# Decoder layer on one core: the first entry's loads in halves, and no idle products between its transposes

## The chip, the cores and the metric

The kernel runs on one core of a Trainium2 chip. The metric is the time of one execution on the device, in microseconds (us). The core has engines that work side by side, each on its own row of instructions: TensorE (PE) for matrix products, VectorE (DVE), ScalarE (ACT), GpSimd (POOL), and SyncE (SP), which here only issues DMAs. ACT issues a few DMAs too. PE loads its stationary operand with a separate instruction, shown as PEld, which overlaps the products. The line numbers below are those of the profile of the kernel before.

## The reference

One decoder layer with B = 4 entries of the batch, 512 rows each, D = 512 and 16 heads of 32, all in float32. Cut to what matters:

```python
x = x + attention(layernorm(x), q_w, q_b, k_w, k_b, v_w, v_b, o_w, o_b)   # causal
x = x + cross_attention(layernorm(x), ctx, ctx)                           # causal, no weights
x = x + ffn(layernorm(x), W_up, W_down, W_gate, W_expert)
# ffn: relu(x @ W_up.T) @ W_down.T + (sum of the softmaxed top-2 gates) * (x @ W_expert)
```

For the first projection of an entry, the rows are normalised (mean and variance over D), and q = xn @ q_w.T + q_b, k = xn @ k_w.T + k_b. The change concerns only how the first entry gets there.

## The kernel before, in words

An entry is 512 x 512 and is held in four row blocks of 128 (NT = 4); the weights are held with the contracted dimension on the partitions in four chunks of 128 (NC = 4). Everything stays on one core, and the four entries follow one another. PE, DVE, ACT and POOL run in exactly the order in which the program writes their instructions (`manual_schedule`, line 947); SP issues the DMAs in program order too, and a DMA may have to wait until an earlier one has landed, because eight completion semaphores are used in turn.

The start, ahead of the loop over entries:

1. `load_x(0)` (lines 70 to 76) issues four DMAs, one per block of 256 KB: blocks 0 and 2 from SP, 1 and 3 from ACT. Then SP issues wq and wk, each in two pieces by row chunks (`load_w(..., 2)`, lines 85 to 91, 104 and 105), then the biases, wv, the context of entry 0 (cv), wo, wup, wdown, wgate, wexp.
2. POOL makes constants, `ident` (the unit matrix) among the first. PE runs `keep_warm("warm", 12)` (line 949, products at line 179), which multiplies `ident` by itself 12 times into a scratch PSUM tile. Nobody reads it.
3. `norm_in(0, x0)` (line 558): for each block, `stats` (lines 189 to 201: `bn_stats` and `bn_aggr` on DVE, then on POOL `ve` and `rstd` as a power of -0.5), and after all four of them `normal` for each block (line 206 on DVE).
4. `turn(0)` and `turn(2)` (line 573) call `columns` (line 245): the transposes of two blocks, four instructions each (line 251), into one PSUM tile of two banks, and then one ACT copy of both (line 257) into `xnT`, the transposed normalised rows. For the first entry `columns` calls `keep_warm` with 2 ahead of each block's four transposes.
5. `query_key(e)` (line 590): for each feature block f of 128, four products for query (line 235, 128 x 512) and four for key, then ACT adds the biases (lines 604 and 607). For the first entry, f = 0 is done in two halves of the rows: `half(n)` (line 615) multiplies 256 columns of `xnT` by wq's chunks and then by wk's; the first half needs only the first ACT copy of step 4.

The first four of these steps (`skip`, line 958: two halves of f = 0, query and key of f = 1) run ahead of attention; the others are the filler that `with_maxima` (line 865) puts between the score products of the first attention. There DVE also reads `xin`, the blocks of the next entry, which SP loads after the weights. Float32 products appear in the profile as two PE instructions each; a transpose is one.

PSUM tiles come from one pool of four buffers (`pair`, line 65), used in turn.

```python
    def keep_warm(name, count):
        out = pair(name)
        for n in range(count):
            nc.tensor.matmul(
                out[:, 0, :P], lhsT=ident, rhs=ident, start=True, stop=True
            )
```

Of the kernel before, what the change touches and what calls it, by code (L numbers as in the profile page):

```python
# [9 lines left out]
F32 = mybir.dt.float32  # L10
# [8 lines left out]
P = 128  # L19
# [7 lines left out]
def decoder_layer(  # L27
# [21 lines left out]
    nc = tc.nc  # L49
    B, S, D = x.shape  # L50
# [3 lines left out]
    NC = D // P  # L54
# [4 lines left out]
    const = ctx.enter_context(tc.tile_pool(name="const", bufs=1))  # L59
# [5 lines left out]
    def pair(name):  # L65

        return ps.tile([P, 2, S], F32, tag="ps", name=name)


    def load_x(b):  # L70
        xb = act.tile([P, NT, D], F32, tag="x", name=f"x_{b}", bufs=2)
        src = x[b].rearrange("(t p) d -> p t d", p=P)
        for t in range(NT):
            queue = nc.scalar if b == 0 and t % 2 else nc.sync
            queue.dma_start(out=xb[:, t, :], in_=src[:, t, :])
        return xb

    def load_cv(b):
# [3 lines left out]
            nc.sync.dma_start(out=cv[:, t, :], in_=src[:, t, :])  # L82
        return cv

    def load_w(ap, name, parts=1):
        w = const.tile([P, NC, ap.shape[-1]], F32, tag=name, name=name)
        src = ap.rearrange("(c p) o -> p c o", p=P)
        for n in range(parts):
            c = slice(n * NC // parts, (n + 1) * NC // parts)
            nc.sync.dma_start(out=w[:, c, :], in_=src[:, c, :])  # L90
        return w

    def load_b(ap, name):
# [7 lines left out]
        return t  # L101

    x0 = load_x(0)
    wq_sb = load_w(wq, "wq_sb", 2)
    wk_sb = load_w(wk, "wk_sb", 2)
    bk_sb = load_b(bk, "bk_sb")
    bq_sb = load_b(bq, "bq_sb")
    wv_sb = load_w(wv, "wv_sb")
# [27 lines left out]
    for r in range(HG):  # L136
# [8 lines left out]
    warm = const.tile([P, 1], F32, name="warm")  # L145
# [14 lines left out]
        out=nfloor,  # L160
        in_=nfloor,
# [7 lines left out]
    parts = []  # L169
    for n in range(2):  # L170
        t = const.tile([P, NT, P], BF16, name=f"parts{n}")
# [3 lines left out]
# [7 lines that stand above are left out]
# [60 lines left out]
            if c < NC - 1:  # L242
                yield

    def columns(srcs, dst, t, tp, scale=None, warm=0):

        for n, src in enumerate(srcs):
            if warm:
                keep_warm(f"warm_{t}_{n}", warm)
            for c in range(NC):  # L250
                nc.tensor.transpose(  # L251
                    tp[:, n, c * P : (c + 1) * P], src[:, c * P : (c + 1) * P], ident
                )
        to = dst[:, :, t * P : (t + 2) * P].rearrange("p c (n q) -> p c n q", q=P)
        come = tp.rearrange("p n (c q) -> p c n q", q=P)
        if scale is None:
            nc.scalar.copy(to, come)
        else:
            nc.scalar.mul(to, come, scale)
# [298 lines left out]
    def norm_in(b, given=None):  # L558

        e = Entry()  # L560
        e.b, e.x, e.xn_t = b, given, None
        src = x[b].rearrange("(t p) d -> p t d", p=P)

        def source(t):
            if given is not None:
                return given[:, t, :]
            xi = work.tile([P, D], F32, tag="xin", name=f"xin_{b}_{t}")
            nc.sync.dma_start(out=xi, in_=src[:, t, :])
            return xi

        made, norms = layernorms(source, f"a{b}", ahead=given is not None)

        def turn(t):
            if e.xn_t is None:
                e.xn_t = act.tile([P, NC, S], F32, tag="xn_t", name=f"xnT_{b}")
            columns(
                [made[t], made[t + 1]],
                e.xn_t,
                t,
                pair(f"tp_a{b}_{t}"),  # L580
                warm=0 if b else 2,
            )

        return e, norms, [(lambda t=t: turn(t)) for t in (0, 2)]
# [5 lines left out]
    def query_key(e):  # L590
        b, made = e.b, {}
        e.q_t = act.tile([P, NC, S], F32, tag="q_t", name=f"qT_{b}")
        e.k_t = act.tile([P, NC, S], F32, tag="k_t", name=f"kT_{b}")

        def query(f):
            made[f] = pair(f"pm_qk{b}_{f}")
            yield from project_t(made[f][:, 0, :], wq_sb, e.xn_t, f)

        def key(f):
            yield from project_t(made[f][:, 1, :], wk_sb, e.xn_t, f)  # L600
            out(f)

        def out(f):
            nc.scalar.activation(
                e.k_t[:, f, :], made[f][:, 1, :], AF.Identity, bias=bk_sb[:, f : f + 1]
            )
            nc.scalar.activation(
                e.q_t[:, f, :],
                made[f][:, 0, :],
                AF.Identity,  # L610
                bias=bqs_sb[:, f : f + 1],
                scale=SCALE,
            )

        def half(n):

            if n == 0:
                made[0] = pair(f"pm_qk{b}_0")
            rows = slice(n * S // 2, (n + 1) * S // 2)
            for u, w in enumerate((wq_sb, wk_sb)):  # L620
                for c in range(NC):
                    nc.tensor.matmul(
                        made[0][:, u, rows],
                        lhsT=w[:, c, :P],
                        rhs=e.xn_t[:, c, rows],
                        start=(n == 0 and c == 0),
                        stop=(n == 1 and c == NC - 1),
                        skip_group_check=True,
                    )
            if n == 1:  # L630
                out(0)

        steps = [(lambda f=f, w=w: w(f)) for f in range(NC) for w in (query, key)]
        if b == 0:
            steps[:2] = [lambda: half(0), lambda: half(1)]
        return steps

    def value(e):
# [308 lines left out]
    with tc.manual_schedule(engines=BY_HAND):  # L947
        e, norms, turns = norm_in(0, x0)
        keep_warm("warm", 12)
        run(norms)  # L950
        run(turns)
        nc.gpsimd.tensor_scalar(bqs_sb, bq_sb, SCALE, None, ALU.mult)
        nc.vector.tensor_reduce(
            fold, ident.rearrange("p (c e) -> p e c", e=HD), axis=AX.X, op=ALU.add
        )
        add_bias(e)
        between_self = query_key(e) + value(e)
        skip, between_cross, ahead = 4, [], []
        for b in range(B):
            more = b + 1 < B  # L960
            sa = Attention(e.q_t, e.k_t, e.v, False, f"s{b}")
            norms, turns = [], []
            if more:
                after, norms, turns = norm_in(b + 1)
            late = with_maxima(between_self, sa, skip, norms)
            if b == B - 1:
                e.x = load_x(b)
            attend(sa, late)
            if b > 0:
                add_bias(e)  # L970
            made = out_projection(e, sa, context(e) + turns)
            steps = (query_key(after) if more else []) + between_cross
            run(steps[:2])
            norm_cross(e, made, 0)
            run(steps[2:3])
            norm_cross(e, made, 2)
            ca = Attention(e.cq_t, e.ck_t, e.cv, True, f"c{b}")
            ca.e, ca.out = e, e.beh_t
            late = with_maxima(steps[3:], ca)
            if b + 2 < B:  # L980
                after.x = load_x(b + 1)
            attend(ca, late)
            if more:
                cvs[b + 1] = load_cv(b + 1)
            filler = value(after) if more else ahead
            run(filler[:1])
            made = add_cross(e, ca)

            fill = matmuls(filler[1:])
            for t, k in ((0, 8), (2, 2)) if b != B - 2 else ((0, 12), (2, 0)):  # L990
                for _ in range(k):
                    next(fill)
                norm_ffn(e, made, t)
            for _ in fill:
                pass
            gates, ups, downs, experts = ffn(e)
            if b + 3 < B:
                between_self, between_cross = gates[:1] + ups + gates[1:] + downs, experts
            elif b + 2 < B:
                between_self, between_cross = gates[:1] + ups + gates[1:] + downs, []  # L1000
                ahead = experts
            elif more:
                between_self, ahead = ahead + ups[:2], experts
                between_cross = gates[:1] + ups[2:] + gates[1:] + downs
            else:
                run(gates[:1] + ups + gates[1:])
                run(downs[:2] + experts[:2] + downs[2:] + experts[2:])
            skip = 0
            if more:
                e = after  # L1010
# [48 lines left out]
```

## Time and profile before

| | us |
|---|---|
| median of 3 runs (809.56 to 809.82) | 809.8 |
| the profiled execution, its own time | 809.92 |
| its span, first to last instruction | 808.2 |
| PE busy | 796.8 |
| DVE busy | 563.7 |
| ACT busy | 395.4 |
| POOL busy | 332.8 |
| first instruction of PE | 1.52 |
| first product of query (line 622) | 11.59 |
| first attention's first score products (line 286) | 27.18 |

The span is the time between the first and the last instruction of one execution under the profiler; the execution's own time is 1.7 us longer. Starts are counted from the beginning of the span. In the rows of a timeline the first number is the start, the second the busy time, then come engine, line, operation, the tile written and the tiles read, their shapes, the number of merged instructions, and in brackets how long the engine had been idle and what ended that. The busy time of a PE row includes the pipeline's tail, so rows that follow each other overlap a little: the distance between starts is the better measure of what a product costs. The trace records the landing of each DMA and its single packets as well; where it is said that a DMA landed so many us after its issue, that is from its row in the table of DMA issues.

### The profile page before, as it was taken

The numbers are of one execution on the slowest core, as the hardware profiler recorded it, in microseconds if no ns is written. First come the engines' busy times: TensorE is split into PE (matmuls) and PEld (weight loads), VectorE is DVE, ScalarE is ACT, GpSimd is POOL, SyncE is SP. The second block draws the span as 40 slices with busy tenths as digits, with TensorE's granted clock in tenths as the row PEclk, the third lists the DMA queues.
The fourth block names the chain that finished last, engine by engine and source line by source line (L and its number), as shares of the span: only waits on it lengthen the run. The fifth ranks groups of instructions, "written<-read, shape, count | busy, mean of one in ns | idle before, by whom it ended". The sixth has DMA issues, their size and how long they took to land. (4 is left out here: it accounts for less than half of the span.)

```text
span 808.2 us, 13950 instructions
## 1 busy us (share of the span) xinstructions
PE 796.8 (99%) x5616; PEld 379.9 (47%) x5616; DVE 563.7 (70%) x957; ACT 395.4 (49%) x448; POOL 332.8 (41%) x523
## 2 busy tenths in 40 slices
PE   8999999999999999999999999999999999999998
PEld 7444454444444454444544445444444454434444
DVE  2478865879678854588867786688859766988512
ACT  2457526861546515566045752686056824674110
POOL 4334612554234732266333482266423653465100
PEclk9999999999999999999999999999999999999999
DMA  9601000001001000020100000000102000000101
GB/s 337 236 28 28 1 1 1 2 2 53 1 27 27 2 1 0 2 77 29 53 14 14 1 2 1 0 2 1 54 26 79 2 2 0 1 2 2 52 1 52
DMA packets 13680, 24.50 MB, mean 30 GB/s; under 512 B 1968, under 2 KB 2224, under 8 KB 13616
## 3 DMA queue, kind: packets, MB, share of 16 engines
q1 hardware_dynamic: 13184, 22.96, 8.4%
q8 instruction: 44, 0.72, 0.4%
q10 hardware_dynamic: 432, 0.66, 0.2%
q14 instruction: 20, 0.16, 0.1%
HBM read 19.42 MB, written 4.19 MB: 29 GB/s over the span
## 5 line engine op out<-in xcount | busy, mean ns | idle before, releaser
L317 DVE TENSOR_REDUCE nm_s<-s_s 128x2 f32<-128x1024 f32 (+3 forms) x128 | 97.0, 811 | 35.2 <-POOL s_s L305 35.2
L317 DVE TENSOR_REDUCE nm_c<-s_c 128x2 f32<-128x1024 f32 (+3 forms) x128 | 95.8, 810 | 31.0 <-POOL s_c L305 31.0
L297 ACT COPY s_s<-sm_s 128x1024 f32<-128x1024 f32 x80 | 77.1, 1015 | 70.7 <-PE sm_s L286 36.4
L297 ACT COPY s_c<-sm_c 128x1024 f32<-128x1024 f32 x80 | 77.1, 1016 | 35.9 <-PE sm_c L286 16.2
L305 POOL TENSOR_SCALAR_AFFINE_SELECT s_c<-s_c 128x512 f32<-128x512 f32 (+1 forms) x80 | 43.9, 550 | 100.4 <-ACT s_c L297 100.4
L305 POOL TENSOR_SCALAR_AFFINE_SELECT s_s<-s_s 128x512 f32<-128x512 f32 (+1 forms) x80 | 43.8, 551 | 97.1 <-ACT s_s L297 97.1
L423 ACT ACTIVATE pt_c<-sc_c 128x1024 f32<-128x1024 f32 x64 | 61.7, 1031 | 21.0 <-PE sc_c L400 15.4
L510 DVE TENSOR_TENSOR sum_s<-sum_s,pt_s 128x256 f32<-128x256 f32 (+2 forms) x72 | 59.8, 895 | 16.7 <-PE pv_s L462 16.7
L431 POOL TENSOR_SCALAR_AFFINE_SELECT pt_c<-pt_c 128x512 f32<-128x512 f32 (+1 forms) x64 | 51.1, 806 | 27.0 <-ACT pt_c L423 26.6
L223 PE MATMUL pm_d<-wdown_sb,hT 128*128 128x512 f32 x128 | 61.5, 610 | 0.0
L423 ACT ACTIVATE pt_s<-sc_s 128x1024 f32<-128x1024 f32 x56 | 53.9, 1030 | 12.6 <-PE sc_s L400 7.0
L235 PE MATMUL pm_u<-fT,wup_sb 128*128 128x512 f32 x128 | 59.3, 604 | 0.0
L223 PE MATMUL pm_v<-wv_sb,xnT 128*128 128x512 f32 x128 | 58.8, 600 | 0.0
L687 PE MATMUL pm_o<-wo_sb,oT_s 128*128 128x512 f32 x128 | 57.8, 596 | 0.0
L235 PE MATMUL pm_qk<-xnT,wk_sb 128*128 128x512 f32 x120 | 57.3, 607 | 0.0
L389 PE MATMUL sc_c<-cqT,ckT 32*128 32x384 f32 (+3 forms) x512 | 56.0, 464 | 1.4 <-ACT sum_c L423 0.8
L235 PE MATMUL pm_qk<-xnT,wq_sb 128*128 128x512 f32 x120 | 56.7, 604 | 0.0
L223 PE MATMUL pm_e<-wexp_sb,fT 128*128 128x512 f32 x120 | 56.3, 604 | 0.0
L389 PE MATMUL sc_s<-qT,kT 32*128 32x128 f32 (+3 forms) x512 | 54.4, 462 | 1.2 <-ACT sum_s L423 0.9
L431 POOL TENSOR_SCALAR_AFFINE_SELECT pt_s<-pt_s 128x512 f32<-128x512 f32 (+1 forms) x56 | 48.1, 868 | 17.6 <-ACT pt_s L423 17.0
L286 PE MATMUL sm_c<-ckT,cqT 32*128 32x512 f32 (+3 forms) x512 | 47.5, 460 | 0.0
L286 PE MATMUL sm_s<-kT,qT 32*128 32x512 f32 (+3 forms) x512 | 47.0, 461 | 0.0
(164 smaller groups left out, 1269.3 us busy)
## 6 DMA issues: line engine op xcount, KB each, us to landing
cv<-in_ctx_dram SPq DMA_DIRECT2D x16, 256.0 KB, 4.0
out_dram<-x SPq DMA_DIRECT2D x15, 256.0 KB, 2.0
x<-in_x_dram SPq DMA_DIRECT2D x14, 256.0 KB, 4.1
xin<-in_x_dram SPq DMA_DIRECT2D x12, 256.0 KB, 2.7
wq_sb<-in_wq_dram SPq DMA_DIRECT2D x2, 512.0 KB, 6.2
wk_sb<-in_wk_dram SPq DMA_DIRECT2D x2, 512.0 KB, 7.8
wv_sb<-in_wv_dram SPq DMA_DIRECT2D x1, 1024.0 KB, 8.3
wo_sb<-in_wo_dram SPq DMA_DIRECT2D x1, 1024.0 KB, 9.7
```

The lines of the kernel that those rows point to most:

```text
L223: nc.tensor.matmul(pm, lhsT=lhs_t[:, c, t * P : (t + 1) * P], rhs=w[:, c, :], start=(c == 0), stop=(c == NC - 1),)
L235: nc.tensor.matmul(pm, lhsT=w[:, c, f * P : (f + 1) * P], rhs=rhs_t[:, c, :], start=(c == 0), stop=(c == NC - 1),)
L286: nc.tensor.matmul(scs[r // 2][:, r % 2, c : c + (i + 1) * P], lhsT=self.q_t[h, g, i * P : (i + 1) * P], rhs=self.k_t[h, g, : (i + 1) * P] ...
L297: nc.scalar.copy(s, scs[n])
L305: nc.gpsimd.affine_select(out=diagonal, in_=diagonal, compare_op=ALU.is_ge, fill=NEG, base=0, pattern=[[0, 2], [0, len(pieces)], [-1, P]], ...
L317: nc.vector.tensor_reduce(self.nm[g][:, i, 2 * n : 2 * n + 2], made[n][:, :, c : c + (i + 1) * P], axis=AX.X, op=ALU.max, negate=True,)
L389: nc.tensor.matmul(scs[r // 2][:, r % 2, c : c + S - j * P], lhsT=self.k_t[h, g, j * P : (j + 1) * P], rhs=self.q_t[h, g, j * P :], start= ...
L423: nc.scalar.activation(pt, scs[n], AF.Exp)
L431: nc.gpsimd.affine_select(out=diagonal, in_=diagonal, compare_op=ALU.is_ge, fill=0.0, base=0, pattern=[[0, 2], [0, len(pieces)], [1, P]], ...
L510: nc.vector.tensor_tensor(to, to, pts[n][:, :, c : c + S - j * P], ALU.add)
L687: nc.tensor.matmul(pms[t // 2][:, t % 2, :], lhsT=a.out[:, c, t * P : (t + 1) * P], rhs=wo_sb[:, c, :], start=(c == 0), stop=(c == NC - 1),)
```

## The change

- Blocks 0 and 1 of the first entry's x are each loaded by two DMAs of 256 columns (128 KB), the left half from SP, the right half from ACT. Blocks 2 and 3 are loaded whole, from SP and from ACT.
- wq and wk are loaded by column halves, in the order wq left, wk left, wq right, wk right. The left half has the columns of f = 0 and 1.
- The idle products between the transposes go; the 12 ahead of them stay.
- For f = 0 only query is done in two halves of the rows; key is done whole, as for the other f. There are five steps ahead of attention instead of four, with the same content.

```diff
         for t in range(NT):
-            queue = nc.scalar if b == 0 and t % 2 else nc.sync
-            queue.dma_start(out=xb[:, t, :], in_=src[:, t, :])
+            if b > 0:
+                nc.sync.dma_start(out=xb[:, t, :], in_=src[:, t, :])
+            elif t > 1:
+                (nc.sync, nc.scalar)[t % 2].dma_start(out=xb[:, t, :], in_=src[:, t, :])
+            else:
+
+                for n, queue in enumerate((nc.sync, nc.scalar)):
+                    half = slice(n * D // 2, (n + 1) * D // 2)
+                    queue.dma_start(out=xb[:, t, half], in_=src[:, t, half])
...
-    def load_w(ap, name, parts=1):
+    def load_w(ap, name):
         w = const.tile([P, NC, ap.shape[-1]], F32, tag=name, name=name)
-        src = ap.rearrange("(c p) o -> p c o", p=P)
-        for n in range(parts):
-            c = slice(n * NC // parts, (n + 1) * NC // parts)
-            nc.sync.dma_start(out=w[:, c, :], in_=src[:, c, :])
+        nc.sync.dma_start(out=w, in_=ap.rearrange("(c p) o -> p c o", p=P))
...
-    wq_sb = load_w(wq, "wq_sb", 2)
-    wk_sb = load_w(wk, "wk_sb", 2)
+
+    wq_sb, wk_sb = (const.tile([P, NC, D], F32, name=name) for name in ("wq_sb", "wk_sb"))
+    for cols in (slice(0, D // 2), slice(D // 2, D)):
+        for w, ap in ((wq_sb, wq), (wk_sb, wk)):
+            nc.sync.dma_start(
+                out=w[:, :, cols], in_=ap.rearrange("(c p) o -> p c o", p=P)[:, :, cols]
+            )
...
-    def columns(srcs, dst, t, tp, scale=None, warm=0):
+    def columns(srcs, dst, t, tp, scale=None):
 
         for n, src in enumerate(srcs):
-            if warm:
-                keep_warm(f"warm_{t}_{n}", warm)
             for c in range(NC):
...
-                warm=0 if b else 2,
...
-            for u, w in enumerate((wq_sb, wk_sb)):
-                for c in range(NC):
-                    nc.tensor.matmul(
-                        made[0][:, u, rows],
-                        lhsT=w[:, c, :P],
-                        rhs=e.xn_t[:, c, rows],
-                        start=(n == 0 and c == 0),
-                        stop=(n == 1 and c == NC - 1),
-                        skip_group_check=True,
-                    )
-            if n == 1:
-                out(0)
+            for c in range(NC):
+                nc.tensor.matmul(
+                    made[0][:, 0, rows],
+                    lhsT=wq_sb[:, c, :P],
+                    rhs=e.xn_t[:, c, rows],
+                    start=(n == 0 and c == 0),
+                    stop=(n == 1 and c == NC - 1),
+                    skip_group_check=True,
+                )
...
-            steps[:2] = [lambda: half(0), lambda: half(1)]
+            steps[:1] = [lambda: half(0), lambda: half(1)]
...
-        skip, between_cross, ahead = 4, [], []
+        skip, between_cross, ahead = 5, [], []
```

## The prediction

> **What bounds the kernel now.** I read the page's busy times first: they say which engine a saving has to reach.
>
> ```profile
> PE 796.8 (99%) x5616; PEld 379.9 (47%) x5616; DVE 563.7 (70%) x957; ACT 395.4 (49%) x448; POOL 332.8 (41%) x523
> ```
>
> PE is idle for only 808.2 - 796.8 = 11.4 us. The same static order runs from the first projection to the end, so whatever lets PE start that row earlier should move the end by as much, if nothing on another engine or a queue arrives too late for the earlier PE. Then the timeline of PE, DVE and ACT over the first 19 us (start, busy time, engine, line, tiles, count, idle before it):
>
> ```profile
> 1.52 5.22 PE L179 MATMUL warm<-ident 128*128 128x128 f32 x28 [1.52 <-POOL ident masks.py:199]
> 8.45 0.66 PE L251 MATMUL tp_a<-ident,xn_a 128*128 128x128 f32 x4 [1.71 <-DVE xn_a L206]
> 8.94 0.61 PE L179 MATMUL warm<-ident 128*128 128x128 f32 x4
> 9.39 0.60 PE L251 MATMUL tp_a<-ident,xn_a 128*128 128x128 f32 x4
> 9.82 0.61 PE L179 MATMUL warm<-ident 128*128 128x128 f32 x4
> 10.27 0.60 PE L251 MATMUL tp_a<-ident,xn_a 128*128 128x128 f32 x4
> 10.71 0.61 PE L179 MATMUL warm<-ident 128*128 128x128 f32 x4
> 11.15 0.60 PE L251 MATMUL tp_a<-ident,xn_a 128*128 128x128 f32 x4
> 11.59 1.89 PE L622 MATMUL pm_qk<-xnT,wq_sb 128*128 128x256 f32 x8
> ...
> 4.66 0.69 DVE L194 BATCH_NORM_STATS2 st_a<-x 128x6 f32<-128x512 f32 x1 [4.66 <-DMA x<-in_x_dram]
> 7.88 2.04 DVE L206 TENSOR_SCALAR xn_a<-x,mv_a,rs_a 128x512 f32<-128x512 f32 x4
> ...
> 10.02 1.01 ACT L257 COPY xnT<-tp_a 128x1024 f32<-128x1024 f32 x1 [6.82 <-PE tp_a L251]
> 11.79 1.01 ACT L257 COPY xnT<-tp_a 128x1024 f32<-128x1024 f32 x1 [0.75 <-PE tp_a L251]
> ```
>
> What the reader should see: DVE starts at 4.66, released by the DMA of x, and then has no idle time; four statistics steps of 0.80 us and the four normalisations follow each other. PE waits 1.71 us for the first normalised block, then runs without a gap, so from 8.45 on it is PE's own work that sets the 11.59, and three of its seven pieces there (8.94, 9.82, 10.71) compute nothing. From 11.59 to 18.50 PE does block 0 of query and key.
>
> Last, the clock, because the idle products touch it. Within the first group (line 179) the starts of single products are 0.213 us apart until about 5.4 us and 0.111 us apart after it. The stretches around the end show the other direction (the PEclk column is the third from the right):
>
> ```profile
> 5.38:8.79 3.41, 1.70 (x15) 1.00 1.05 397
> 8.79:12.21 3.42, 3.42 (x30) 1.00 1.07 371
> 804.10:807.51 3.41, 0.42 (x2) 1.00 0.23 77
> 807.51:808.10 0.59, 0.00 (x0) 0.50 0.00 0
> ```
>
> The clock record goes to full rate at 5.38 us and to half at 807.51: 802.13 us, 235 times 3.413 us, so it is decided in steps of 3.41 us. A step with 0.42 us of PE work ended in half clock, one with 1.70 us (5.38 to 8.79) did not.
>
> **The change, part by part.**
>
> *Idle products.* Sixteen go (two before each of four transpose groups, two instructions each). The first four end the first group and lie in PE's wait for DVE: nothing saved. The other three sets take 0.45, 0.45 and 0.44 us on PE's path, 1.33 us together. Not all of that is gained, since DVE and ACT come next. The single normalisations end at 8.39, 8.85, 9.30 and 9.92 (the fourth starts late, at 9.375, because POOL's rs_a ends at 9.34). A group of four transposes takes 0.44 us and starts 0.06 us after its block. So the groups start at 8.45, 8.94 (behind the first group), 9.38 and 9.98. ACT's first copy started 0.63 us after the start of the second group (9.39 to 10.02), so now 8.94 + 0.63 = 9.57, and with 1.01 us and 0.06 us to PE the first product of query can start at 10.65. The new last arrival is that copy, not PE's last transpose (10.42). The second copy: 9.98 + 0.63 + 1.01 = 11.62, needed after the first half of query, 10.65 + 1.73 = 12.38: covered by 0.76 us. Gain 11.59 - 10.65 = 0.94 us.
>
> *x in halves.* Now blocks 0 and 1 are on two queues that share the DMA engines, and land together: by the packet records block 0's last completion is at 4.27, block 1's at 4.35, and DVE starts 0.40 us after the former. In steady flow a 2 KB packet takes 0.084 us and an engine carries eight for each block, alternating. In halves the first sixteen packets of an engine are all block 0, 1 KB each. The only 1 KB packets of this trace (the last output) take 0.046 us. Sixteen of those save 16 x (0.084 - 0.046) = 0.6 us against sixteen of 2 KB; slow first packets (0.3 to 1.0 us) stay. Block 0 would be usable at about 4.1. Block 1 comes 16 x (2 x 0.046 - 0.084) = 0.13 us later than now, at about 4.9, and its statistics would be due at 4.9. Block 2's last completion is at 5.40, usable at 5.80, with the same 0.13 us 5.93; due at 6.29 - 0.6 = 5.7. So block 2 becomes the late one, and the chain gains 6.29 - 5.93 = 0.36 to 6.29 - 5.80 = 0.49 us. I take 0.40. Ends: 0 if slow first packets are paid per packet (sixteen either way), 0.6 if block 2 comes earlier too. Below nothing is bounded by block 1: were it 0.3 us later than reckoned, it still starts before 5.49.
>
> Here a rule speaks against the change: the Trainium skill, "DMA: Bandwidth & Descriptors", section "Issuing engines are not separate DMA queues", says that DMAs of different issuing engines run on the same 16 engines and interleave, and that issuing from several saves only sequencer time. By that rule the halves give nothing, and the sum is 0.97. The two completions 0.09 us apart show the interleaving; but both kernels use two queues, and what changes is which bytes go first. So I keep 0.40.
>
> *Weights by column halves.* Before, query's block 0 needs all of wq (landed at 8.8); now half of it, behind the same 1.5 MB, which is where the first wq piece lands now: 1.70 + 5.7 = 7.4. Even 0.5 us later that is early for 10.25. wk's first half takes the place of the piece that landed at 8.8 and is needed at 13.7. Second halves are needed at about 24. PE did not wait for weights before, so nothing is gained; cover 2.3 us and more.
>
> *SP and ACT queues.* SP issues one DMA more ahead of the weights (0.43 us) and ACT one more (0.43 us) ahead of its table load; ACT is idle until 9.5. In the built order the second column half of wq now waits for the first half of block 0 of x, that of wk for the other half, about 3.9 to 4.1 us. Behind them queue the biases, wv and cv. By 4.2 the engines have moved 0.6 MB of the 2 MB issued ahead, so none runs dry. The tightest later user is the next entry's xin, which lands at 21.34 + 9.9 = 31.2 and is read by DVE at 32.50, then about 31.1. With 2.5 MB now in 1 KB packets it may land up to 0.6 us later, so DVE may stand up to 0.8 us. Behind it stand four maxima of line 317; DVE has 0.56 us idle right after, and nothing on PE waits for them for two units. I take 0.
>
> *Query in two halves, key whole.* 8 x 0.216 x 2 + 8 x 0.43 = 6.88 us, where four halves took 6.91: 0.03. Two attention units later PE's order is the same as before, line for line. The four removed scratch tiles are one full turn of the four PSUM buffers, so the later tiles meet the same ones.
>
> Sum: 0.94 + 0.40 + 0.03 = 1.37 us. The profiled execution took 809.92 (span 808.2 and 1.7 around it), so 808.55; the median 809.8 lies 0.12 lower: 808.4.
>
> **The clock: the other rule against it.** The Trainium skill, "TensorE: Matmul & The Clock Gate", section "Part 4: PE-mode transpose", says that transposes do not count as PE-busy the way matmuls do. In this trace the step from 5.38 to 8.79 holds 1.19 us of idle products and 0.34 us of transposes, and kept the clock. Changed, the products end at 6.13, so that step would hold 0.75 us of products and 0.77 us of transposes: 1.52 against 1.53 if both count, 0.75 if only products do, between the 0.42 that lost the clock and the 1.19 that kept it. By the rule a stretch from 6.1 to 10.2 holds nothing that counts, more than one step. At half clock a step of full PE work loses 1.7 us. So: 808.4 by the row, 810.1 or worse by the rule. I take the row, since no step of this trace shows transposes failing to count, and keep the other as a rival.
>
> **Rivals.**
>
> *The products go, x is no earlier.* 0.97 us: 808.8. For it: slow first packets. Against it: 0.046 against 0.084 us.
>
> *One step at half clock* from about 9 to 10 on: 1.7 - 1.37 = 0.3 lost: 810.1. For it: the rule, and the lull of 1.9 us that stays ahead of the transposes. Against it: 44% of the step is busy in total, as now.
>
> *Slower:* the same half clock, but it holds for a second step, because the step in which it falls is half transposes and so doesn't bring the clock back. Then PE pays 3.4 us: 809.8 - 1.37 + 3.4 = 811.8. It decides once more than 1.37 us, that is 2.7 us of PE's work, is done at half clock. The first group at 0.213 us, which needed from 1.52 to 5.38 to get out of it, speaks for how long that takes.
>
> *DVE or POOL as the new bound:* already in the sum (POOL's rs_a delays the fourth block); it costs only the third of the three sets.
>
> **How the numbers follow.** Clean gain, 808.1 to 808.8, centre 808.4: 0.60. No earlier x, 808.8: 0.13. One step cold, 809.6 to 810.3: 0.12. Two steps, 811.4 to 812: 0.12. Something larger: 0.03. 0.2% is 1.6 us, about what a measurement here tells from no change: faster means under 808.2, slower over 811.4. The clean case reaches under 808.2 only at its end (0.6 us for x), and with a few tenths between executions I give that a quarter of it: faster 0.2, slower 0.13, same 0.67. The range goes from 807.9 to 810.3 and leaves out the second step.
>
> **What would show it.** In the profile after: DVE's first statistics near 4.1 to 4.2, with a gap ahead of the third; transposes in groups of 0.44 us without line 179 between; the first query product near 10.2; key's block 0 ending near 17.1; PE without a gap after it. Products of 256 columns 0.216 us apart mean full clock; 0.43 us means the cold rivals. A DVE start still at 4.66 means the first rival. I am wrong if the gain is there at 18 us and gone at 100 us: then a later wait took it.

## The result and the profile after

The changed kernel takes 810.93 us (median of 20 executions, 809.41 to 813.32) beside 809.67 us for the kernel before in the same job: ratio 1.0016 [1.0009, 1.0023], so 1.26 us are lost where 1.4 were forecast as a gain. The profiled execution took 810.22 us, with a span of 808.3 and 1.9 around it. It is one of the 6 executions whose mean granted clock is 0.999 or more (809.41 to 810.22); the other 14, at 0.995 to 0.998, took 810.47 to 813.32. The median of the six is 809.93, so most of the 1.26 us is clock. Two losses have to be found: one that the profile shows at full clock, and one of clock that it doesn't.

First the busy times. PE has 24 instructions fewer than before: 16 of the idle products, and 8 because key of f = 0 is done whole. It is busy for only 0.4 us less, since the clock came up at 7.69 us (before: 5.38), so that the idle products that stay ran at half clock to their end.

```profile
PE 796.4 (99%) x5592; PEld 377.2 (47%) x5592; DVE 564.3 (70%) x957; ACT 395.4 (49%) x448; POOL 333.1 (41%) x523
```

The timeline of PE over the first 19 us:

```profile
1.52 5.49 PE L188 MATMUL warm<-ident 128*128 128x128 f32 x24 [1.52 <-POOL ident masks.py:199]
9.08 2.19 PE L258 MATMUL tp_a<-ident,xn_a 128*128 128x128 f32 x16 [2.07 <-DVE xn_a L215]
11.30 3.72 PE L627 MATMUL pm_qk<-xnT,wq_sb 128*128 128x256 f32 x16
14.85 3.60 PE L244 MATMUL pm_qk<-xnT,wk_sb 128*128 128x512 f32 x8
18.29 1.02 PE L244 MATMUL pm_qk<-xnT,wq_sb 128*128 128x512 f32 x2
```

From the first transpose to the first product of query it is now 2.22 us (11.30 - 9.08), where it was 3.14 (11.59 - 8.45): 0.92 saved, and 0.94 was reckoned. But the transposes start 0.63 us later than before, not 0.40 earlier. DVE says why:

```profile
3.84 0.69 DVE L203 BATCH_NORM_STATS2 st_a<-x 128x6 f32<-128x512 f32 x1 [3.84 <-DMA x<-in_x_dram]
4.67 0.68 DVE L203 BATCH_NORM_STATS2 st_a<-x 128x6 f32<-128x512 f32 x1
5.57 0.69 DVE L203 BATCH_NORM_STATS2 st_a<-x 128x6 f32<-128x512 f32 x1
7.68 0.69 DVE L203 BATCH_NORM_STATS2 st_a<-x 128x6 f32<-128x512 f32 x1 [1.20 <-DMA x<-in_x_dram]
8.51 2.05 DVE L215 TENSOR_SCALAR xn_a<-x,mv_a,rs_a 128x512 f32<-128x512 f32 x4
```

Block 0 comes 0.82 us earlier than before (3.84 against 4.66), but DVE waits 1.20 us for block 3. By the packet records block 3's last completion is at 7.34, where it was at 5.64. The table of DMA issues from 1.65 to 1.9 us holds the last two blocks (line, queue, count, KB, us to landing). Before, they took 4.6 us (SP) and 4.8 us (ACT):

```profile
x<-in_x_dram SPq DMA_DIRECT2D x1, 256.0 KB, 3.9
x<-in_x_dram ACTq DMA_DIRECT2D x1, 256.0 KB, 6.0
```

In the clean profile 0.21 us of the front's gain is still there at 18 us (18.29 against 18.50). It goes at 466 us. ACT's timeline there, first after, then before:

```profile
462.36 1.94 ACT L430 ACTIVATE sum_s<-sc_s 128x1024 f32<-128x1024 f32 x2 [0.86 <-PE sc_s L407]
465.09 1.95 ACT L430 ACTIVATE pt_s<-sc_s 128x1024 f32<-128x1024 f32 x2 [0.79 <-PE sc_s L407]
```

```profile
462.56 1.94 ACT L423 ACTIVATE sum_s<-sc_s 128x1024 f32<-128x1024 f32 x2 [0.86 <-PE sc_s L400]
465.00 1.94 ACT L423 ACTIVATE pt_s<-sc_s 128x1024 f32<-128x1024 f32 x2 [0.50 <-PE sc_s L400]
```

After is 0.20 us ahead at the first row and 0.09 behind at the second: ACT stood 0.29 us longer between the same two pieces, and the next products of probabilities by values follow it (467.44 against 467.35).

A further 0.2 us lies outside the span. In the six kernels of this document that load x by six DMAs (after, e2, e3, e7, e8, e14) an execution takes 1.91 to 1.94 us more than its span on average; in the kernel before and the other nine it is 1.71 to 1.73. Why is not shown.

### The profile page after: what moved, and what is told of

Same layout as the page of the kernel before. It is cut to its first block, busy times and chain, and to the rows that moved or that the text cites. A ratio compares the mean times of both kernels' runs of the same rounds, so it can differ in the third digit from the quotient of the medians.

```text
span 808.3 us, 13907 instructions
## 1 busy us (share of the span) xinstructions
PE 796.4 (99%) x5592; PEld 377.2 (47%) x5592; DVE 564.3 (70%) x957; ACT 395.4 (49%) x448; POOL 333.1 (41%) x523
## 5 line engine op out<-in xcount | busy, mean ns | idle before, releaser
L244 PE MATMUL pm_qk<-xnT,wk_sb 128*128 128x512 f32 x128 | 60.9, 606 | 0.0
```

The costliest lines, as they stand in the source:

```text
L244: nc.tensor.matmul(pm, lhsT=w[:, c, f * P : (f + 1) * P], rhs=rhs_t[:, c, :], start=(c == 0), stop=(c == NC - 1),)
```

## Experiments

All kernels compute the whole output. "Full" is the number of executions with a mean granted clock of at least 0.999. Differences are each run's median less that of the kernel before in its own job.

| kernel | x of the first entry | products: first group, between | median us | less before | ratio, 95% | full |
|---|---|---|---|---|---|---|
| after | halves 0, 1 | 12, none | 810.93 | +1.26 | 1.0016 [1.0009, 1.0023] | 6 of 20 |
| e1_no_idle | whole | 12, none | 810.00 | +0.26 | 1.0000 [0.9992, 1.0008] | 3 of 13 |
| e2_after_idle | halves 0, 1 | 12, 2 each | 812.80 | +3.06 | 1.0032 [1.0020, 1.0044] | 1 of 5 |
| e3_w_rows | halves 0, 1 | 12, none | 811.72 | +1.98 | 1.0020 [1.0012, 1.0028] | 4 of 14 |
| e4_x_whole | whole | 12, none | 809.88 | +0.14 | 0.9999 [0.9991, 1.0007] | 5 of 13 |
| e5_whole_17 | whole | 17, none | 808.78 | -0.81 | 0.9991 [0.9985, 0.9998] | 18 of 21 |
| e6_first14 | whole | 14, none | 808.74 | -0.85 | 0.9992 [0.9984, 1.0000] | 10 of 13 |
| e7_halves_17 | halves 0, 1 | 17, none | 810.22 | +0.63 | 1.0008 [1.0000, 1.0016] | 11 of 13 |
| e8_xrows_17 | row halves 0, 1 | 17, none | 810.46 | +0.87 | 1.0011 [1.0004, 1.0018] | 18 of 21 |
| e9_1k_4dmas | 0 and 1 as two halves | 14, none | 809.30 | -0.48 | 0.9997 [0.9988, 1.0005] | 9 of 11 |
| e10_tiny_dmas | whole, biases behind 0, 1 | 14, none | 809.42 | -0.36 | 0.9998 [0.9989, 1.0007] | 10 of 11 |
| e11_block0_halves | halves 0 | 14, none | 811.25 | +1.47 | 1.0018 [1.0009, 1.0026] | 4 of 11 |
| e12_tiny_sp | whole, biases behind 0 | 14, none | 809.38 | -0.43 | 1.0006 [0.9994, 1.0017] | 7 of 11 |
| e13_tiny_behind | whole, biases behind 2, 3 | 14, none | 808.98 | -0.66 | 0.9993 [0.9985, 1.0002] | 10 of 11 |
| e14_last_halves | halves 2, 3 | 14, none | 809.21 | -0.43 | 0.9994 [0.9985, 1.0003] | 11 of 11 |

The ratios are formed within rounds, so they can differ a little from the quotient of the two medians.

**The parts, one at a time**

*e1_no_idle:* the kernel before without the idle products between transposes.

```diff
-                warm=0 if b else 2,
```

> The kernel before with only the idle products between the transposes gone; loads as before. Theory C (clock): without them some executions do part of the first entry at half clock, so the times spread from about 808.8 to 811.5 with mean granted clocks below 1.000, median within 1 us of before's 809.7 or above it. Rival D (transfers alone made the changed kernel slow and uneven): the times are as tight as before's, 0.94 us faster, near 808.7, all clocks at 1.000.

Measured: 810.00, no gain. Three executions of 13 kept the clock and took 808.86 to 809.01; the other ten took 809.93 to 811.41. The profile is one of those. Its stretches by steps of the clock record (length, PE's busy time and count, granted clock, DMA share, GB/s):

```profile
4.83:8.24 3.41, 1.20 (x11) 1.00 1.05 398
8.24:11.66 3.42, 3.40 (x16) 0.50 1.07 371
11.66:15.07 3.41, 3.41 (x18) 1.00 1.05 387
```

The step before the transposes is 35% full, and the next is at half clock. That next step holds the sixteen transposes and nothing else, as the timeline shows:

```profile
8.26 3.60 PE L251 MATMUL tp_a<-ident,xn_a 128*128 128x128 f32 x16 [2.22 <-DVE xn_a L206]
```

The step that follows is at full clock again. So a step of transposes brings the clock back, and only one step is lost. What follows: removing all four pairs saves PE's time and loses the clock in most executions; some of the pairs did a service.

*e2_after_idle:* the changed kernel with those products again. The diff is the reverse of e1's (and of the two lines in the helper).

> The changed kernel with the idle products between the transposes put back; loads changed. Theory C: the spread of over 3 us goes, clocks at 1.000; what is left is what the late block 3 of x costs, so 809.5 to 810.7. Rival D: the spread stays as in the changed kernel, 809.4 to 813.

Measured: 812.80 (810.52 to 813.71; one execution of five kept the clock). Theory C expected the clock kept and at most 810.7; by the number alone rival D (809.4 to 813) would be right. The profile shows a lost step of the clock nonetheless: block 2's statistics start at 7.03 after a gap of 1.70, and the first transposes at 9.22. The longer wait for x is a longer lull:

```profile
6.09:9.50 3.41, 1.26 (x12) 1.00 1.08 366
9.50:12.92 3.42, 3.42 (x19) 0.50 1.10 349
```

The first pair of products fills 0.45 us of it and isn't enough; then the pairs between are paid for at half clock too.

*e3_w_rows:* the changed kernel with wq and wk by halves of the rows, as before (2 KB packets).

```diff
-    for cols in (slice(0, D // 2), slice(D // 2, D)):
-        for w, ap in ((wq_sb, wq), (wk_sb, wk)):
+    for w, ap in ((wq_sb, wq), (wk_sb, wk)):
+        for c in (slice(0, NC // 2), slice(NC // 2, NC)):
```

> The changed kernel with the weights of query and key by row halves (2 KB packets, as before); x in halves, no idle products. If the 1 KB weight packets hold up block 3 of x: its statistics start at 6.4 to 6.6 us instead of 7.68, DVE's 1.20 us gap shrinks under 0.5, and executions with full clock take about 808.4. If the halves of x hold it up: still near 7.7 us. By theory C the spread stays in both.

Measured: 811.72, and 809.38 to 810.35 where the clock was kept, not 808.4. In the profile, which is the fastest of the fourteen executions, x is still late: 0.70 us of gap ahead of block 2, and block 3's statistics at 6.90, between the two forecasts. So the weights' halves are not the cause of the late x.

*e4_x_whole:* the changed kernel with x in whole blocks.

```diff
-            elif t > 1:
-                (nc.sync, nc.scalar)[t % 2].dma_start(out=xb[:, t, :], in_=src[:, t, :])
-            else:
...
+            queue = nc.scalar if b == 0 and t % 2 else nc.sync
+            queue.dma_start(out=xb[:, t, :], in_=src[:, t, :])
```

> The changed kernel with blocks 0 and 1 of x loaded whole from one queue each, as before; weights by column halves, no idle products. If the 1 KB weight packets hold up block 3 of x: DVE starts at 4.66 us and block 3's statistics still come late (7.5 us or later, before: 7.08). If the halves of x do it: block 3 is on time, 7.08. By theory C the spread stays in both.

Measured: 809.88, and 808.77 to 809.13 where the clock was kept. DVE's statistics start at 4.37, 5.20, 5.99 and 6.79 without a gap, query at 10.37. So the halves of x cost, and what is left over is the clock.

**The lull and the halves, apart**

*e5_whole_17, e6_first14, e7_halves_17:* the idle products are put where the lull is. e5 is e4 with 17 in the first group, e7 is the changed kernel with 17. e6 is e1 with 14: the first pair, but ahead of the transposes' block instead of between.

```diff
-        keep_warm("warm", 12)
+        keep_warm("warm", 14)
```

In e5 and e7 the same line has 17.

> The changed kernel with x in whole blocks, and with 17 idle products in the first group instead of 12; none between the transposes. Theory L (the lull between the first group and the first transposes loses the clock, when a 3.41 us step holds under some 40% of PE work, transposes included): the lull shrinks to about 1.4 us, so nearly all executions keep the clock: 808.6 to 808.9, spread as before's 0.3 us. Rival T (transposes don't count, so the stretch of bare transposes loses it): spread from 808.7 to 811.5 as without the five products.

> The kernel before with the idle products between the transposes gone but the pair ahead of the first transposes kept (14 in the first group); loads as before. Theory L: that pair is what held the clock, so most executions stay near 808.8, with a few slower; median under 809.1. Rival T: as without any of them, median 810.0, most clocks near 0.997.

> The changed kernel with 17 idle products in the first group. Theory L: the clock losses mostly go and what the halves of x cost in landing stays: 809.0 to 810.2, well under the changed kernel's 810.9, and above the same kernel with whole blocks. Rival T: spread to 813 as the changed kernel.

Measured: 808.78, 808.74 and 810.22. One pair of products (e1 to e6) is worth 1.1 us by the differences to before. The kernels with 12 products ran on other chips than those with 14 and 17. But the kernel before, which ran beside each, lost the clock more seldom beside e1 (1 of 35 executions) than beside e6 (7 of 57), and 14 products with x on time mostly kept it on two more chips (e9, e13, e14); so the chip is an unlikely cause. The timeline of PE in e6 (its lost clock step is far from here, see the last section):

```profile
1.52 6.05 PE L179 MATMUL warm<-ident 128*128 128x128 f32 x28 [1.52 <-POOL ident masks.py:199]
8.11 2.19 PE L251 MATMUL tp_a<-ident,xn_a 128*128 128x128 f32 x16 [0.54 <-DVE xn_a L206]
10.32 2.00 PE L621 MATMUL pm_qk<-xnT,wq_sb 128*128 128x256 f32 x8
```

8.11 to 10.32 is 2.21 us: 0.93 saved against before's 3.14, with the lull filled to 0.54. e5 and e6 are the same within 0.04 us, so the weights' halves, the whole key and three more idle products are worth nothing here. e7 less e5 is the price of x in halves alone, on the same chip: 1.44 us by the medians, 1.28 among the executions with full clock. Its DVE waits twice:

```profile
6.14 0.69 DVE L203 BATCH_NORM_STATS2 st_a<-x 128x6 f32<-128x512 f32 x1 [0.93 <-DMA x<-in_x_dram]
7.77 0.69 DVE L203 BATCH_NORM_STATS2 st_a<-x 128x6 f32<-128x512 f32 x1 [0.71 <-DMA x<-in_x_dram]
```

**Why halves make x late**

Candidates: packets of 1 KB, the number of DMAs, a third DMA on ACT's queue, or DMAs issued ahead of the later blocks.

*e8_xrows_17:* e7 with blocks 0 and 1 split by 64 rows, so that packets stay at 2 KB.

```diff
-                    half = slice(n * D // 2, (n + 1) * D // 2)
-                    queue.dma_start(out=xb[:, t, half], in_=src[:, t, half])
+                    half = slice(n * P // 2, (n + 1) * P // 2)
+                    queue.dma_start(out=xb[half, t, :], in_=src[half, t, :])
```

> As the kernel with 17 products and x in halves, but blocks 0 and 1 of x are split by 64 rows instead of 256 columns: the same number of DMAs and bytes in the same order, packets of 2 KB. If the 1 KB packets of x delay blocks 2 and 3: their statistics come without a gap over 0.4 us and it takes about 808.5 to 808.9. If it is the number of DMAs ahead of them: gaps of 0.7 to 1.7 us on DVE as with column halves, 809.0 to 810.2.

Measured: 810.46, with gaps of 0.63, 0.17 and 0.61 us. It doesn't decide: issuing a row half took 0.60 to 0.74 us where a column half takes 0.43 to 0.45, so its later blocks are issued later as well (2.03 and 2.29 us, after: 1.70).

*e9_1k_4dmas* (from here on all are e6 with another load of x or of the biases): blocks 0 and 1 together by two DMAs, left halves from SP, right halves from ACT. 1 KB packets, but four DMAs as before.

```diff
+        if b == 0:
+            for n, queue in enumerate((nc.sync, nc.scalar)):
+                half = slice(n * D // 2, (n + 1) * D // 2)
+                queue.dma_start(out=xb[:, :2, half], in_=src[:, :2, half])
```

> The kernel before, 14 idle products in the first group and none between, with blocks 0 and 1 of x loaded together by two DMAs: left halves of both from SP, right halves of both from ACT. Four DMAs for x as before, but 1 KB packets. Theory K (1 KB packets of x delay blocks 2 and 3): gaps of over 0.4 us ahead of DVE's third or fourth statistics, under 350 GB/s from 3.2 to 6.2 us, time 809.2 or more. Theory N (two more DMAs delay them): no gap, 390 to 400 GB/s, 808.7 to 808.9.

*e10_tiny_dmas:* x whole; the two loads of biases (2 KB) are issued behind blocks 0 and 1, one on each queue.

```diff
+            if b == 0 and t < 2:
+                queue.dma_start(out=(bk_sb, bq_sb)[t], in_=(bk, bq)[t])
```

> The same base (14 idle products, x in whole blocks), with the two bias loads of 2 KB issued behind blocks 0 and 1, one on each queue, so that six DMAs stand for x's four, with 2 KB packets for x. Theory N: blocks 2 and 3 come late, gaps on DVE of over 0.4 us, 809.2 or more. Theory K: no gap, 808.7 to 809.0.

*e11_block0_halves:* only block 0 in halves, five DMAs.

```diff
+            if b == 0 and t == 0:
+                for n, queue in enumerate((nc.sync, nc.scalar)):
+                    half = slice(n * D // 2, (n + 1) * D // 2)
+                    queue.dma_start(out=xb[:, t, half], in_=src[:, t, half])
+                continue
```

> The same base with only block 0 of x in column halves on two queues, blocks 1 to 3 whole: five DMAs, a quarter of x in 1 KB packets. Both theories: between the two, block 0 earlier by 0.3 to 0.8 us, the later blocks delayed by about half of what both halved blocks cost: 808.5 to 809.6. If it is at or under 808.7, halving one block pays.

*e12_tiny_sp:* both biases from SP, between blocks 0 and 2; ACT's queue as before.

```diff
+            if b == 0 and t == 0:
+                queue.dma_start(out=bk_sb, in_=bk)
+                queue.dma_start(out=bq_sb, in_=bq)
```

> The base with 14 idle products and x in whole blocks, both bias loads of 2 KB issued by SP between blocks 0 and 2; ACT's queue has blocks 1 and 3 alone, as before. If any two more DMAs ahead of the later blocks upset the transfers: under 350 GB/s from 3.2 to 6.2 us, a gap on DVE of over 0.4 us, 809.2 or more. If it takes a third DMA on ACT's queue: no gap, near 400 GB/s, 808.7 to 808.9.

*e13_tiny_behind:* the biases behind blocks 2 and 3.

```diff
+            if b == 0 and t > 1:
+                queue.dma_start(out=(bk_sb, bq_sb)[t - 2], in_=(bk, bq)[t - 2])
```

> The base with 14 idle products and x in whole blocks, the two bias loads issued one on each queue behind blocks 2 and 3, ahead of the weights. If the place matters (DMAs issued between x's blocks): no gap on DVE, 390 to 400 GB/s from 3.2 to 6.2 us, 808.7 to 808.9. If the number of DMAs at the start is enough: a gap of over 0.4 us, under 350 GB/s, 809.2 or more.

*e14_last_halves:* blocks 2 and 3 in halves, 0 and 1 whole; six DMAs as in the changed kernel.

```diff
+            if b == 0 and t > 1:
+                for n, queue in enumerate((nc.sync, nc.scalar)):
+                    half = slice(n * D // 2, (n + 1) * D // 2)
+                    queue.dma_start(out=xb[:, t, half], in_=src[:, t, half])
+                continue
```

> The same base with blocks 2 and 3 in column halves on two queues, blocks 0 and 1 whole: six DMAs, the order of bytes as in the base. If only DMAs ahead of a block delay it: block 2 on time, block 3 at most 0.4 us late, 808.7 to 809.1. If the number is enough: uneven landings and gaps as with blocks 0 and 1 in halves, 809.3 or more.

The stretch from 3.2 to 6.2 us shows the rate at which all DMAs together move bytes while x lands (length, PE's clock, DMA share, GB/s; the share sums the packets' times and can pass 1.00). First e6:

```profile
3.20:6.20 3.00, 1.00 1.04 395
```

e9, with 1 KB packets:

```profile
3.20:6.20 3.00, 1.00 1.07 398
```

e14, six DMAs, the small ones last:

```profile
3.20:6.20 3.00, 1.00 1.06 380
```

e12, 2 KB of biases ahead of block 2:

```profile
3.20:6.20 3.00, 1.00 1.06 315
```

And the changed kernel:

```profile
3.20:6.20 3.00, 1.00 1.01 307
```

In each of these rows the DMA engines count as busy all the time, but move up to 22% less than in e6. In e7, e8 and e10 the share itself falls, to 0.86 to 0.93, and the rate to 278 to 322 GB/s.

DVE's gap ahead of a statistics step follows: none in e9, e13 and e14; 0.79 us in e10; 1.06 in e12; 0.62 and 1.70 in e11. So the packet size is innocent of the gaps (e9), a third DMA on ACT isn't needed (e12), and neither number nor halves alone do it (e13 at 359 GB/s, e14 at 380). What the late blocks have in common is that they stand behind smaller DMAs on their queue. In e12 these are on SP's queue alone, and only SP's block 2 is late; block 3, from ACT, is on time and follows without a wait:

```profile
7.25 0.70 DVE L197 BATCH_NORM_STATS2 st_a<-x 128x6 f32<-128x512 f32 x1 [1.06 <-DMA x<-in_x_dram]
8.07 0.66 DVE L197 BATCH_NORM_STATS2 st_a<-x 128x6 f32<-128x512 f32 x1
```

I can name the place, not the mechanism. By the packet records the completions of a block that is on time spread over 0.5 to 0.75 us between the engines (once 1.0, in e6), those of the late ones over 1.2 to 2.4. In e13 and e14 the first piece of wq, which is now what stands behind the small DMAs, spreads over 1.3 to 1.4 us, where it was 0.5 to 0.75 in the kernels without them; nothing waits for it so early. Why the engines drift apart stays open.

Not every forecast of time was met. e9 took 809.30 us, where 808.7 to 808.9 was expected if packets cost nothing. It has no gap, but each of its two first DMAs carries a half of both blocks, so block 0 is usable only at 4.97 us (e6: 4.33), and query starts at 10.96 (e6: 10.32):

```profile
4.97 0.69 DVE L198 BATCH_NORM_STATS2 st_a<-x 128x6 f32<-128x512 f32 x1 [4.97 <-DMA x<-in_x_dram]
```

e10 (809.42) and e12 (809.38) fell where they should if two more DMAs upset the later blocks. e13 took 808.98 at 359 GB/s, a little outside what was expected if the place matters (808.7 to 808.9, 390 to 400 GB/s), and e14's 809.21 lies between its two ranges.

e11 (811.25) missed what both theories gave it, 808.5 to 809.6. Its profile joins both losses, with the clock's steps as for e1: the late block 3 makes a lull with 22% in one step, and the transposes run at half clock.

```profile
6.54:9.95 3.41, 0.75 (x7) 1.00 1.04 386
9.95:13.36 3.41, 3.39 (x16) 0.50 1.04 376
```

e13 and e14 have x in time and still end 0.2 to 0.4 us behind e6 by the differences to before. They have the pause at 466 us, as has every kernel here with one more DMA issued by ACT (after, e2, e3, e7, e8, e10, e11); in e1, e4, e5, e6, e9 and e12 ACT issues as many as before and the pause is not there. The cause of the pause was not tried. In e14 the 0.2 us outside the span come on top.

## Why the prediction failed, step by step

The sum by runs, each against before in its own job: e5, all but the halves of x and with the lull filled, -0.81; x in halves (e7 less e5) +1.44; the short first group (after less e7) +0.63. Together +1.26; that they add up is no proof, since the runs in between cancel. It says how the loss divides.

*Idle products.* The term of 0.94 held: 0.92 in the profile after, 0.93 in e6. The step that failed is the sentence "The first four end the first group and lie in PE's wait for DVE: nothing saved". Nothing saved is right, but removing this pair cost something: it was work in the lull, the idle stretch between the first group and the first transposes. Without it 10 of 13 (e1) and 14 of 20 executions (after) have a clock below 0.999; with it or more in the first group, 3 of 13 (e6, in the profiled one of them not at the entry, see below) and 3 of 21 (e5). These six look alike: a clock of 0.998, and 1.5 to 1.7 us above those with full clock, where nine of e1's ten have 0.996 or 0.997 and eight of them are 1.0 to 1.2 us above. So perhaps none of the six lost its step at the entry; no profile of the other five shows it.

*The clock.* The prediction compared one step of one profile, 1.52 against 1.53 us from 5.38 to 8.79 (counted by the distances of starts; by busy time, as its row shows, before's step has 1.70). Its own finding was that the clock is decided in steps of 3.41 us. One stretch of 802.13 us could not show that, but the runs do: e1's half-clock record lasts 3.41 us and the full one behind it 795.31, 233 times as long. What the prediction did not ask is where the steps lie in other executions. The Trainium skill says it in "TensorE: Matmul & The Clock Gate", section "What's actually happening": the window runs freely and doesn't reset when a kernel starts. The profiles agree: full clock starts at 4.83, 5.38, 6.09 and 7.69 in e1, before, e2 and after. A lull has to be good for every position of the steps. In e1's profile the step ended 0.02 us ahead of the first transpose, so it held idle products alone, 1.20 us where the prediction had 1.52. In after's profile the position was kind, and both steps were well filled (the first row's clock column reads 1.00 only because the clock record begins at 7.69; the products in it are 0.213 us apart):

```profile
4.27:7.69 3.42, 2.74 (x13) 1.00 1.01 314
7.69:11.10 3.41, 2.02 (x16) 1.00 1.10 362
```

In all sixteen profiles the steps that lost the clock at the entry were 22 to 37% full (e11, e1, e2: 0.75, 1.20, 1.26 of 3.41 us). In the other thirteen the emptiest step at the entry, from the first full clock on, was 49 to 86% full. It is the step that counts, not the length of the lull: e10 kept the clock over a lull of 2.75 us, longer than e1's 2.22, because its step was half full:

```profile
4.74:8.15 3.41, 1.69 (x15) 1.00 0.96 333
```

*Row against rule.* That transposes don't count was rightly set aside: e1's step of nothing but transposes brought the clock back, and after's second step above, which holds transposes alone and is 59% full, kept it. The measurement decides against the page's section "Part 4: PE-mode transpose" for these float32 transposes. For the cold rival the prediction named the rule and also the lull of 1.9 us, and then set the lull aside with "44% of the step is busy in total, as now". That holds for one position of the steps only. At others the lull loses the clock, so "One step at half clock" was the right mechanism. Its price of 1.7 us was too high: e1's executions with a lost step mostly take about 1.1 us more than its three with full clock, and the way from the first transpose to query is 1.2 us longer in e1's profile than in e6's (3.44 against 2.21). And its 810.1 still counted on an earlier x. "Slower", with a second step, is not seen in any profile: e1's step full of transposes brings the clock back. But three of after's twenty executions, with clocks of 0.995 and 0.996 (812.32 to 813.32), must have lost two steps by this estimate: one step lowers the mean clock by 0.5 x 3.41 / 808 = 0.002, and the profiles of e1 and e11, with one lost step and the half clock of the end, stand at 0.997. Where the two were lost isn't shown.

*x in halves.* Block 0 was usable at 3.84, even before the reckoned 4.1. The step that failed is "Below nothing is bounded by block 1": only block 1's delay was bounded, and blocks 2 and 3 were moved by 0.13 us, for packet times alone. They were issued half a microsecond later, behind two more DMAs, and block 3 completed 1.70 us later. That packets of 1 KB are quick was right (0.046 us in after as well). The term was +0.40, and -1.44 measured. Of the 1.50 us between the profiled executions of e7 and e5, 1.0 is query's start (11.38 against 10.38), 0.3 the pause at 466 us and 0.2 lies outside the span. The rule weighed there, that issuing engines share the DMA engines and gain only sequencer time ("DMA: Bandwidth & Descriptors", "Issuing engines are not separate DMA queues"), put the gain at 0; that was nearer, but no bound either. The late x also stretches the lull, so this step feeds the other (e2, e11).

*Weights by column halves, SP and ACT queues.* The weights at nothing: right (e5 and e6 within 0.04). The queues at nothing: one more DMA on ACT goes with 0.2 to 0.3 us at 466 us, and two more for x with 0.2 us outside the span, which no row of before could show.

*Query in two halves, key whole.* 0.03 reckoned; 6.99 us from query's first product to f = 1 (18.29 - 11.30) against 6.91, so -0.08. e6 takes 7.01 with four halves (17.33 - 10.32), so this is not the whole key's doing. Too small to matter. Two slips of the reckoning are as small: its products add up to 6.90, not 6.88, and a quarter of the clean case's 0.60 is 0.15, not 0.2.

## What to carry to other kernels

An idle product is worth something only where it fills a lull; elsewhere it costs its time. Look for the lull by steps of the clock and at every position of those steps, which takes many executions and not one profile. Hastening the first block of a load by cutting it up can make the later blocks late when the small DMAs are issued ahead of them on the same queue; look at the last block, not at the first. Here the best versions keep x whole and put all idle products in the first group, none between the transposes: 808.74 us with 14 (ratio 0.9992 [0.9984, 1.0000]) and 808.78 with 17 (0.9991 [0.9985, 0.9998]), which can't be told apart.

## What the runs showed of the hardware

In e6's profile the clock is lost once more, far from the entry, after a step 70% full of products on 32 rows or 32 columns of the array; 7 of 57 executions of before in that job have a clock of 0.998 too and took 810.98 to 811.30, but there is no profile of one, so the place is not shown for them.

```profile
710.27:713.69 3.42, 2.38 (x34) 1.00 0.03 7
713.69:717.10 3.41, 3.41 (x16) 0.50 0.00 0
```

How full the step was doesn't explain it, and neither does the share of the array: in before's profile a step at the same place, as full and with the same kinds of products, kept the clock, and so did steps 69 to 72% full there in five other profiles. What sets e6's apart stays open.

```profile
711.93:715.34 3.41, 2.37 (x30) 1.00 0.00 0
```

A step at the start that was 81% full of cold products (0.86 to 4.27 in after, counted back from the first full clock) didn't raise the clock; the next one, 80% full, did.
